# The routing gate of the last row: one load ahead of time, gated in operations of 512, in a two-layer block on one core

## The chip, the cores and the metric

The kernel runs on one core of a Trainium2 chip. Its time is the device time of one execution in microseconds (us), and runs of the same kernel are compared by their median. The core has five engines with a queue each: TensorE (PE, with its weight loads shown as PEld), VectorE (DVE), ScalarE (ACT), GpSimd (POOL) and SyncE (SP). SP computes nothing; it issues most of the transfers between device memory and the on-chip buffers.

## The reference, cut to what matters

Four rows (batch entries) of 512 tokens with 512 channels pass through two layers. Ahead of each of the four sublayers the input is gated by a bidirectional recurrence over a side input:

```python
x = x + L0_attn(L0_cond(x, f, f, w, u, cond))     # state-space mixer
x = x + L0_ffn(L0_cond2(x, f, f, w, u, cond))     # mixture of 8 experts, top 2
x = x + L1_attn(L1_cond(x, f, f, w, u, cond))     # causal attention
x = x + L1_ffn(L1_cond2(x, f, f, w, u, cond))     # dense feed-forward

# _bi_wkv(r, k, v, ...): all but the sigmoid depends on the side input only
base = sigmoid(r) * (num / maximum(den, 1e-8))
out = base * (0.8 + 0.2 * tf)

# L0_ffn: routing from the gated input, then the experts
logits = x @ gate_w.T + gate_b
top_vals, top_idx = top_k(logits, 2)
routing = softmax(top_vals)
```

So a gate (everything but `sigmoid(r)`) can be made long before its input is known. The kernel writes the sigmoid as a tanh: `h = (tanh(x / 2) + 1) * g`, where the half is in `g`.

## The kernel before, in words

Channels lie on the 128 partitions, in four chunks (`NC`), and tokens along the free dimension; a row in this form is a buffer of 128 x 4 x 512. `make_gates` computes the gates of all rows and sublayers piece by piece on DVE and ACT and stores them in device memory (`gts[l][b]`). `gated` (line 393) takes a buffer from a pool, loads a gate or a range of its tokens into it on SP's queue (line 397), and has `apply_gate` (line 379) turn it into the gated input in place: for each chunk a tanh of x on ACT into a scratch buffer `th`, then one DVE operation that adds one and multiplies (line 385).

The state-space mixer runs row by row (`for b`), within a row over four tiles of 128 tokens (`for t`). In a tile, `start_tile` computes z from the row's gated input `w.h` (line 1096), `load_sums` loads the decays `lm` (line 1126), `decays` and `outputs` do the scan, and a tile later `squares`, `norm`, `turn` and `project` (line 1244) finish it, and `add_x` (line 1260) adds the result to the row's x, for the tokens of that tile only. The gated input of rows 1 and 3 is in pool `hp` under the tag `h`, a single buffer; row 3's is read for the last time by the z matmuls of its tile 3, which are issued while tile 2 is worked on.

The routing of row b, `choose_experts` (line 605), runs during the mixer of row b + 1. It gates the row in parts into `h1` (also in `hp`, a single buffer), and for each part `logits` (line 480) computes the logits (`pl`, line 485), turns h to token rows on PE (`pht`, line 501), copies them to a scratch buffer `hr` (line 505) and stores them as `rows_h` for the experts to gather. Rows 0 to 2 are done in two parts of 256 tokens, the last row in four parts of 128, since each of its tiles becomes available only when its mixer is done. `th`, `hr` and the scratch of `route` and `order_blocks` all share one tag of the pool `tmp`, with two buffers. `route` then ranks the experts and counts; `order_blocks` lists blocks of 128 tokens of one expert.

The experts (`Experts.round`: `pg` line 788, `pn` line 799, `po` line 821, with flips `pfl` line 759 and `pyt` line 812) work on such blocks. Their first rounds, for blocks of rows 0 to 2, begin in the last tile of row 3, so that the last parts of row 3's routing, its last mixer tile and expert rounds are on PE together. After that come the remaining rounds, attention (to line 1689) and the dense feed-forward.

Order of work: the program order gives the priorities; a planner then lists the instructions of each engine in the order in which it believes them ready, by its own costs, and every engine and every queue works through its list in order. `with after(...)` and the table bookkeeping (`act.use`) only forbid some instructions to be listed before others.

Of the kernel before, what the change touches and what calls it, by code (L numbers as in the profile page):

```python
# [10 lines left out]
F32 = mybir.dt.float32  # L11
I32 = mybir.dt.int32
AF = mybir.ActivationFunctionType
ALU = mybir.AluOpType
# [3 lines left out]
P = 128  # L18
B, T, C = 4, 512, 512
NC = C // P  # L20
NT = T // P
# [61 lines left out]
def block_kernel(ctx: ExitStack, tc: tile.TileContext, a: dict, out: bass.AP):  # L83
    nc = tc.nc
# [47 lines left out]
    act = Tables()  # L132
# [9 lines left out]
    def ps_mm(name):  # L142
        return ps.tile([P, 512], F32, tag="mm", name=name, bufs=4)
# [37 lines left out]
    th = const.tile([P, B], F32, name="th")  # L181
# [32 lines left out]
    gts = [[dr.tile([P, NC, T], F32, name=f"g{l}_{b}") for b in range(B)] for l in range(4)]  # L214
# [156 lines left out]
    def pump(n=1, until=None):  # L371
        for _ in range(n):
            while until not in made and not next(making, True):
                pass
# [3 lines left out]

    def apply_gate(g, xs):

        for cc in range(NC):
            th = tmp.tile([P, T], F32, tag="th", name="th")
            n = xs.shape[-1]
            act(th[:, :n], xs[:, cc, :], AF.Tanh, scale=0.5)
            nc.vector.scalar_tensor_tensor(
                g[:, cc, :], th[:, :n], 1.0, g[:, cc, :], ALU.add, ALU.mult
            )

    def have(gate):
        while gate not in made:  # L390
            pump()

    def gated(l, b, xb, pool, part=slice(0, T), **kw):
        have((l, b))
        n = part.stop - part.start
        g = pool.tile([P, NC, n], F32, **kw)
        nc.sync.dma_start(out=g, in_=gts[l][b][:, :, part])
        apply_gate(g, xb[:, :, part])
        return g
# [202 lines left out]
        nc.vector.tensor_tensor(v2, v2, v1, ALU.mult)  # L602
        yield

    def choose_experts(b, xb, parts, pool, fine=False, **kw):

        lg = rt.tile([P, NT, E], F32, tag="lg", name="lg", bufs=2)
        nt = NT // parts
        for i in range(parts):
            h = gated(1, b, xb, pool, slice(i * nt * P, (i + 1) * nt * P), **kw)  # L610
            if fine:
                yield
            logits(h, b, lg, i * nt, nt)
            yield
        yield from route(lg, b, fine, pool, **kw)
# [258 lines left out]
    with ExitStack() as ph:  # L874
# [4 lines left out]
        hp = ph.enter_context(tc.tile_pool(name="ssm_h", bufs=1, reuse_waits="tile"))  # L879
        sm = ph.enter_context(tc.tile_pool(name="ssm", bufs=1, reuse_waits="tile"))  # L880

        def load_x(b):
            xb = (hp if b % 2 else even).tile([P, NC, T], F32, tag="x", name=f"x{b}")
            nc.sync.dma_start(out=xb, in_=a["xT"][:, b, :].rearrange("(c p) t -> p c t", p=P))
            return xb
# [35 lines left out]
        x = {0: load_x(0)}  # L921
# [164 lines left out]
        def start_tile(w, t):  # L1086
            u = Tile_()
            u.w, u.t = w, t
            u.tok = slice(t * P, (t + 1) * P)
            u.first, u.last = t == 0, t == NT - 1  # L1090

            u.zs = []
            for hh in range(2):
                pz = ps_mm("pz")
                for k in range(NC):
                    nc.tensor.matmul(
                        pz,
                        lhsT=w.h[:, k, u.tok],
                        rhs=wzt[:, k, hh * 512 : (hh + 1) * 512],
                        start=(k == 0),  # L1100
                        stop=(k == NC - 1),
                    )
                zs = sm.tile([P, 512], F32, tag="zs", name="zs", bufs=3)
                act(zs, pz, AF.Silu)
                u.zs.append(zs)
            return u
# [161 lines left out]
        def rounds(n):  # L1268
            for _ in range(n):
                if moe.i < min(NEARLY, moe.known):  # L1270
                    moe.round()
# [34 lines left out]
        routing = iter(())  # L1306
        for b in range(B):
            if b + 1 < B:
                x[b + 1] = load_x(b + 1)
            if b:  # L1310
                routing = choose_experts(
                    b - 1, x[b - 1], 2, hp, fine=True, tag="h1", name="h1", bufs=1
                )
            for t in range(NT):
                last = t == NT - 1
                exps = act.LOG_EXP
                if b == B - 1 and t >= NT - 2:
                    exps = act.EXP
                if b == B - 1 and t == NT - 2:
                    have(last_gates)  # L1320
                    for _ in making:
                        pass
                    early.close()
                    moe.open()
                    act.use(exps)
                pump(1, last_gates)
                if not last:
                    load_sums(w, t + 1, 0)
                elif b + 1 < B:
                    load_sums(following, 0, 0)  # L1330
                decays(u, 1)
                rounds(1)
                if t == NT - 2 and b + 1 < B:
                    start_scan(following)
                outputs(u, 0)
                if last and b + 1 < B:
                    more_x(following, NDI)
                with after(nc.scalar, nc.gpsimd):
                    if old is not None:
                        squares(old, 1)  # L1340
                pump(1, last_gates)
                with after(nc.vector, nc.gpsimd):
                    if old is not None:
                        norm(old)
                pump(1, last_gates)
                with after(*ENGINES):
                    if old is not None:
                        turn(old)

                if t >= 2:  # L1350
                    with after(*ENGINES):
                        next(routing, None)
                if t == NT - 3 and b + 1 < B:
                    have((0, b + 1))
                if t < 2 and b:
                    have((1, b - 1))
                if b + 1 < B or not last:
                    act.use(act.SILU)
                if t < 2:
                    with after(*ENGINES):  # L1360
                        next(routing, None)
                if t == NT - 3 and b + 1 < B:
                    following = start_row(b + 1)
                if b + 1 < B and t == NT - 2:
                    silu(following.Bc)
                    silu(following.Cc)
                if b + 1 < B and last:
                    for c in following.xc:
                        silu(c)
                nxt = None  # L1370
                if not last:
                    nxt = start_tile(w, t + 1)
                elif b + 1 < B:
                    w = following
                    nxt = start_tile(w, 0)
                act.use(exps)
                rounds(1)
                if nxt is not None:
                    start_scores(nxt)
                pump(1, last_gates)  # L1380
                with after(nc.tensor):
                    if old is not None:
                        project(old)
                if b + 1 < B and t == NT - 2:
                    with after(nc.tensor):
                        sums(following)
                if nxt is not None:
                    load_sums(w, nxt.t, 1)
                    decays(nxt, 0)
                with after(nc.scalar):  # L1390
                    if old is not None:
                        scale(old)
                outputs(u, 1)
                rounds(1)
                with after(nc.tensor, nc.vector):
                    if old is not None:
                        add_x(old)
                with after(nc.scalar, nc.gpsimd):
                    squares(u, 0)
                pump(1, last_gates)  # L1400
                with after(*ENGINES):
                    next(routing, None)
                    if b == B - 1 and t < 2:
                        next(routing)
                if b == B - 1 and t == NT - 2:
                    order_blocks(0, NEARLY)
                    moe.know(NEARLY)
                old, u = u, nxt
        act.leave()
        routing = choose_experts(B - 1, x[B - 1], 4, hp, tag="h1", name="h1", bufs=1)  # L1410
        for _ in range(NT - 1):
            next(routing)
        squares(old, 1)
# [11 lines left out]
    x = []  # L1425
    for b in range(B):
        xb = xpool.tile([P, NC, T], F32, name=f"xr{b}")
# [266 lines left out]
    with ExitStack() as ph:  # L1694
# [9 lines left out]
        for b in range(B):  # L1704
            h = gated(3, b, x[b], gp, tag="h", name=f"h3_{b}")
# [101 lines left out]
```

## Time and profile before

Three runs took 2554.86, 2562.75 and 2564.61 us.

| | us |
|---|---|
| median of the runs | 2562.75 |
| profiled execution | 2560.14 |
| its span | 2558.4 |
| mixer with gates and first routings, to about | 620 |
| row 3's routing beside the first expert rounds | 650 to 760 |
| experts, to about | 1158 |
| attention and dense feed-forward | the rest |

The profiled execution's time holds the span and what lies around it (1.7 us). A line of a timeline has the start in us from the span's start, the length, the engine, the source line, the operation and what it writes and reads; in square brackets stands the idle time before it and who ended it. A line of waits has who waited, for whom, the total in us, how often, and the longest. In the lines by stage stand the stage, its length, and then for PE, PEld, DVE, ACT and POOL the busy time and the number of instructions, the clock granted to PE, the share of the transfer engines and GB/s.

### The profile page before, as it was taken

The page shows a single profiled execution, that of the slowest core. Times are in us where ns is not written, and L with a number is a line of the kernel's source. Part 1 is how long each engine was busy: PE and PEld are TensorE (multiplying, and loading weights), DVE is VectorE, ACT ScalarE, POOL GpSimd, SP SyncE. Part 2 cuts the span into 40 slices and gives each one's busy share as a digit, 9 for nine tenths or more (in the row PEclk, how much of TensorE's full clock was granted, in tenths as well). Part 3 has the DMA queues.
Part 4 walks back from the last instruction along what each step waited for, and adds up shares of the span by engine and source line. Part 5 has one row for each costly group of instructions (what it writes and reads, how often), then busy time and mean ns, then how long its engine had stood idle before and what let it go on. Part 6 is the DMA issues. An engine that isn't in the chain of part 4 may idle for free.

```text
span 2558.4 us, 24369 instructions
## 1 busy us (share of the span) xinstructions
PE 2420.2 (95%) x8146; PEld 1288.4 (50%) x8146; DVE 1402.9 (55%) x2771; ACT 1012.0 (40%) x2074; POOL 271.9 (11%) x306
## 2 busy tenths in 40 slices
PE   3879999999999899998999999999999999999999
PEld 1545655656544444444555555555555544444444
DVE  8789999896335667646666555555444441010010
ACT  4576767667123343424544443444333331000000
POOL 4022423213211111110000000000000000000000
PEclk9989999999999999999999999999999999999999
DMA  6232524324244598775111111110000021000000
GB/s 215 71 104 71 185 75 136 120 83 153 79 169 140 195 331 319 264 262 206 58 37 46 46 33 34 46 33 9 9 17 17 17 107 46 17 4 13 9 8 17
DMA packets 88190, 243.04 MB, mean 95 GB/s; under 512 B 9472, under 2 KB 19072, under 8 KB 78976
## 3 DMA queue, kind: packets, MB, share of 16 engines
q1 hardware_dynamic: 79200, 215.78, 24.1%
q0 software_dynamic: 6560, 21.50, 2.5%
q10 hardware_dynamic: 2304, 4.20, 0.4%
q8 instruction: 65, 1.06, 0.2%
q14 instruction: 61, 0.50, 0.1%
HBM read 276.43 MB, written 46.53 MB: 126 GB/s over the span
## 4 chain that ended last, share of the span: by engine, by line
PE 49%; DVE 4%; ACT 2%; DMA 0%; issue 0%; ACTq 0%; SPq 0%; DVEq 0%
PE pd L1642 8%; PE pq L1578 7%; PE pfu L1716 6%; PE pfo L1726 6%; PE pfg L1711 6%; PE pctx L1627 5%; PE psc L1595 4%; PE pv L1564 2%; PE ptp L1618 2%; PE pk L1556 2%; DVE nmax L1600 1%; DVE psc L1598 0%; ACT pr L127 0%; DVE num L258 0%; DVE den L258 0%; DVE den L264 0%
## 5 line engine op out<-in xcount | busy, mean ns | idle before, releaser
L1578 PE MATMUL pq<-h,wq 128*128 128x512 f32 x512 | 245.3, 593 | 0.0
L1642 PE MATMUL pd<-cx,wd 128*128 128x512 f32 x512 | 222.4, 592 | 0.0
L1025 PE MATMUL pc<-h,wxb 128*128 128x512 f32 x320 | 150.3, 626 | 43.3 <-DVE h L1284 39.4
L1598 DVE TENSOR_TENSOR psc<-psc,mask 128x128 f32<-128x128 f32 x256 | 72.1, 287 | 205.2 <-PE psc L1595 205.2
L127 ACT ACTIVATE hd<-pfg,cols 128x512 f32<-128x512 f32 x44 | 30.2, 687 | 382.4 <-PE pfg L1711 382.4
L1721 DVE SCALAR_TENSOR_TENSOR hd<-pfu,cols,hd 128x512 f32<-128x512 f32 x44 | 33.0, 750 | 269.4 <-PE pfu L1716 269.3
L127 ACT ACTIVATE pr<-psc,nmax 128x128 f32<-128x128 f32 (+3 forms) x256 | 135.2, 529 | 91.8 <-DVE nmax L1600 91.4
L1716 PE MATMUL pfu<-h,ffu 128*128 128x512 f32 x352 | 158.7, 592 | 0.8 <-DMA ffu<-in_upT 0.8
L1711 PE MATMUL pfg<-h,ffg 128*128 128x512 f32 x352 | 158.9, 593 | 0.0
L788 PE MATMUL pg<-w,hT 128*128 128x512 f32 x296 | 142.6, 625 | 14.4 <-DMA w<-in_w1x 9.4
L1627 PE MATMUL pctx<-pT,v 128*128 128x512 f32 (+3 forms) x512 | 152.2, 440 | 3.9 <-ACT pT L1621 2.1
L1642 PEld LDWEIGHTS pd<-cx,wd 128*128 128x128 f32 x512 | 96.1, 190 | 114.8 <-issue 111.0
L1595 PE MATMUL psc<-kT,qT 128*128 128x128 f32 (+3 forms) x512 | 150.6, 434 | 1.6 <-ACT qT L1586 0.9
L1726 PE MATMUL pfo<-hd,ffd 128*128 128x512 f32 x352 | 151.7, 592 | 0.0
L1650 DVE TENSOR_TENSOR xr<-xr,pd 128x512 f32<-128x512 f32 x64 | 44.0, 687 | 190.8 <-PE pd L1642 190.8
L821 PE MATMUL po<-w,yT 128*128 128x512 f32 x296 | 137.0, 603 | 7.6 <-DMA w<-in_w2x 7.0
L1627 PEld LDWEIGHTS pctx<-pT,v 128*128 128x128 f32 x512 | 94.6, 191 | 92.7 <-issue 41.5
L799 PE MATMUL pn<-w,hT 128*128 128x512 f32 x296 | 133.5, 593 | 0.0
L1586 ACT ACTIVATE qT<-pq 128x512 f32<-128x512 f32 x64 | 38.2, 596 | 235.8 <-PE pq L1578 221.4
L1600 DVE TENSOR_REDUCE nmax<-psc 128x1 f32<-128x128 f32 (+3 forms) x256 | 123.7, 484 | 3.1
L1025 PEld LDWEIGHTS pc<-h,wxb 128*128 128x128 f32 x320 | 62.3, 199 | 115.8 <-issue 73.9
L1618 PEld LDWEIGHTS ptp<-ident,pr 128*128 128x128 f32 x640 | 77.3, 141 | 80.2 <-issue 38.7
(316 smaller groups left out, 4233.7 us busy)
## 6 DMA issues: line engine op xcount, KB each, us to landing
w<-in_w1x SPq DMA_DIRECT2D x76, 1024.0 KB
w<-in_w2x SPq DMA_DIRECT2D x38, 1024.0 KB
wb<-in_b1x SPq DMA_DIRECT2D x38, 512.0 KB
lm<-cs SPq DMA_DIRECT2D x32, 512.0 KB
kt<-in_fT SPq DMA_DIRECT2D x62, 256.0 KB
ek<-ek SPq DMA_DIRECT2D x62, 256.0 KB
ekv<-ekv SPq DMA_DIRECT2D x62, 256.0 KB
g<-num SPq DMA_DIRECT2D x30, 512.0 KB
```

The source lines that it names most:

```text
L127: nc.scalar.activation(*args, **kw)
L788: nc.tensor.matmul(pg, lhsT=hT[:, k, :], rhs=self.w1[s][0][:, k, :], start=(k == 0), stop=(k == NC - 1))
L821: nc.tensor.matmul(po, lhsT=yT[:, j, :], rhs=self.w2[s][:, j, :], start=(j == 0), stop=(j == NI - 1))
L1025: nc.tensor.matmul(pc, lhsT=wxb[:, k, m * P : (m + 1) * P], rhs=h[:, k, :], start=(k == 0), stop=(k == NC - 1),)
L1578: nc.tensor.matmul(pq, lhsT=u.wq[:, k, i * KVC : (i + 1) * KVC], rhs=u.h[:, k, :], start=(k == 0), stop=(k == NC - 1),)
L1595: nc.tensor.matmul(psc[:, :n], lhsT=qT[:, qi * P : n], rhs=u.kT[:, :n], start=True, stop=True)
L1600: nc.vector.tensor_reduce(nmax, psc[:, :n], AX.X, ALU.max, negate=True)
L1627: nc.tensor.matmul(pctx[:, kj * P :], lhsT=u.v[:, kj, :], rhs=pT[:, kj, kj * P :], start=(kj == 0), stop=(kj == NT - 1),)
L1642: nc.tensor.matmul(po, lhsT=u.wd[:, i, m * P : (m + 1) * P], rhs=u.ctxT[i], start=(i == 0), stop=(i == HPG - 1),)
L1711: nc.tensor.matmul(pg, lhsT=wg[:, k, cs], rhs=h[:, k, :], start=(k == 0), stop=(k == NC - 1))
L1716: nc.tensor.matmul(pu, lhsT=wu[:, k, cs], rhs=h[:, k, :], start=(k == 0), stop=(k == NC - 1))
L1726: nc.tensor.matmul(po, lhsT=wdn[:, i, m * P : (m + 1) * P], rhs=hd[i], start=(i == 0), stop=(i == NFF - 1),)
```

## The change

Two things are edited. `apply_gate` no longer goes by chunks in all cases: where a part has 256 or 128 tokens, one operation covers all four chunks of 128 tokens (a strided view of 4 x 128), so that every operation has 512 elements in a partition. A part of 256 tokens then takes two operations on each engine where it took four, a part of 128 tokens one where it took four; whole rows are treated as before.

For the last row, the gate is loaded whole (1 MB) into the buffer of tag `h` of `hp`, which row 3's own gated input held. The load is written at the end of tile 2 of row 3, after the z matmuls of tile 3 and ahead of the load of the second half of that tile's decays (`load_sums(w, nxt.t, 1)`). `choose_experts` then gates each part in place in that buffer; it takes no `h1` buffer and issues no load for this row.

```diff
     def apply_gate(g, xs):
 
-        for cc in range(NC):
+        n = xs.shape[-1]
+        for i in range(NC * n // T):
+            at = (slice(None), i) if n == T else (slice(None), slice(None), slice(i * P, (i + 1) * P))
             th = tmp.tile([P, T], F32, tag="th", name="th")
-            n = xs.shape[-1]
-            act(th[:, :n], xs[:, cc, :], AF.Tanh, scale=0.5)
-            nc.vector.scalar_tensor_tensor(
-                g[:, cc, :], th[:, :n], 1.0, g[:, cc, :], ALU.add, ALU.mult
-            )
+            tv = th if n == T else th.rearrange("p (k t) -> p k t", t=P)
+            act(tv, xs[at], AF.Tanh, scale=0.5)
+            nc.vector.scalar_tensor_tensor(g[at], tv, 1.0, g[at], ALU.add, ALU.mult)
...
-    def choose_experts(b, xb, parts, pool, fine=False, **kw):
+    def choose_experts(b, xb, parts, pool, fine=False, gate=None, **kw):
...
-            h = gated(1, b, xb, pool, slice(i * nt * P, (i + 1) * nt * P), **kw)
+            part = slice(i * nt * P, (i + 1) * nt * P)
+            if gate is None:
+                h = gated(1, b, xb, pool, part, **kw)
+            else:
+                h = gate[:, :, part]
+                apply_gate(h, xb[:, :, part])
...
                     nxt = start_tile(w, 0)
+                if b == B - 1 and t == NT - 2:
+
+                    last_gate = hp.tile([P, NC, T], F32, tag="h", name="h1_last")
+                    nc.sync.dma_start(out=last_gate, in_=gts[1][B - 1])
                 act.use(exps)
...
-        routing = choose_experts(B - 1, x[B - 1], 4, hp, tag="h1", name="h1", bufs=1)
+        routing = choose_experts(B - 1, x[B - 1], 4, hp, gate=last_gate)
```

## The prediction

> **What bounds the kernel now.** I read the page's busy table first, then the waits of TensorE (PE) in the stretch in which the last row hands over to the experts, then the timelines of PE, SyncE (SP), ScalarE (ACT) and VectorE (DVE) there, and last the lines by form.
>
> ```profile
> span 2558.4 us, 24369 instructions
> PE 2420.2 (95%) x8146; PEld 1288.4 (50%) x8146; DVE 1402.9 (55%) x2771; ACT 1012.0 (40%) x2074; POOL 271.9 (11%) x306
> ```
>
> PE is busy for 2420.2 of 2558.4 us: 138 us of idle time is all that can be won without taking PE work away, and the change takes none away. So the question is which PE idle time ends earlier. The busy time by stage around the last row shows one bad slice and a slow one after it:
>
> ```profile
> 680.00:700.00 20.00, 20.00 (x54) 9.26 (x53) 4.75 (x7) 3.73 (x8) 5.11 (x7) 1.00 0.34 121
> 700.00:720.00 20.00, 15.43 (x62) 9.00 (x61) 7.30 (x19) 3.75 (x11) 4.22 (x11) 0.94 0.45 153
> 720.00:740.00 20.00, 20.00 (x68) 11.10 (x67) 3.60 (x9) 5.76 (x12) 1.00 (x1) 0.89 0.39 145
> ```
>
> The first column after the length is PE's busy time, the third from the end the granted clock. From 700 to 720 us PE idles 4.57 us, and the clock is 0.94 and then 0.89. PE's waits from 640 to 740 us say for whom:
>
> ```profile
> PE pl L485 <- DVE h L385: 4.6, 1, 4.6
> PE pfl L759 <- DMA hb<-rows_h,idx_h: 1.8, 2, 1.4
> PE pyd L1180 <- DVE xdt L1154: 0.8, 1, 0.8
> ```
>
> One wait, 4.6 us long, of the routing logits for the gated input h. PE's timeline has it, and what follows:
>
> ```profile
> 713.60 0.42 PE L501 MATMUL pht<-ident,h 128*128 128x128 f32 x2
> 718.58 0.60 PE L485 MATMUL pl<-gw,h 128*128 128x8 f32 x2 [4.57 <-DVE h L385]
> ...
> 721.03 1.11 PE L812 MATMUL pyt<-ident,u 128*128 128x128 f32 x4
> 721.94 1.06 PE L759 MATMUL pfl<-ident,hb 128*128 128x128 f32 x4
> ...
> 725.03 0.60 PE L1235 MATMUL pyt<-ident,y 128*128 128x128 f32 x4
> ```
>
> Four transposes take 1.11 and 1.06 us just after the wait and 0.60 us at 725.03: PE runs at half speed for a while. What the logits wait for is part 2 of the last row's gate, loaded into the only h1 buffer once part 1's transposes have read it (here the lines of SP, DVE and ACT, each from its own timeline):
>
> ```profile
> 715.16 0.54 SPq L397 DMA_DIRECT2D h<-g  x1
> ```
> ```profile
> 718.23 0.49 DVE L385 SCALAR_TENSOR_TENSOR h<-th,h 128x128 f32<-128x128 f32 x2 [3.38 <-DMA h<-g]
> ```
> ```profile
> 703.37 0.58 ACT L505 COPY hr<-pht 128x512 f32<-128x512 f32 x1 [4.04 <-PE pht L501]
> 703.85 0.31 ACT L123 ACTIVATE th<-x 128x128 f32<-128x128 f32 x1
> 706.12 0.31 ACT L123 ACTIVATE th<-x 128x128 f32<-128x128 f32 x1 [1.96 <-DMA rows_h<-hr]
> ```
>
> The load takes 3.07 us from 715.16 to DVE's start at 718.23; nothing of it is covered. The ACT lines show a second queue: hr and th share a ring of two buffers, and part 1's second tanh waits until hr has been written to memory.
>
> **Part 1: the whole load, a tile ahead.** Gone are four loads of 256 KB (SP, 0.53 to 0.58 us of issue each); added is one of 1 MB. It waits for the h slot, which row 3's own input frees after the last z matmul of tile 3 (line 1096, 632.71 + 3.60 = 636.3 us). At the 319 GB/s of the page's fast slices 1 MB takes 3.3 us, and with 2.2 us around it (256 KB took 3.07 us, of which 0.8 at that rate) it lands near 642 us, an estimate. The part-0 gating starts at 656.61 us today, part 1 at 703.85, so the load has 14 us to spare. On SP the next work after its 626 us load of decays is at 649.70 (the old first load) and 657.80 us (expert weights): nothing stands behind it if it is issued at 636 us. [...] But the row shows the planner issuing by readiness: the old part-0 load (written after the experts' first round) went out at 649.70, ahead of that round's weights at 657.80. [...]
>
> When can the parts be gated? The tanh tiles come from the th ring, and its tiles seem to be handed out in the order written: part 0's first tanh ran at 656.61 us, right after the ring's last tile of the block ordering (DVE line 682, 656.01), though x of tile 0 had been ready since 624.2. So I expect no earlier start for part 0, and part 1's tanh only after part 0's hr, near 703.9, as now. From there a part is: hr 0.58, tanh 0.63 (128x512 form, line 123), gating 0.675 (128x512 form of line 385), logits 0.81, transposes 0.43, and five hand-overs of the 0.16 us that the timeline shows between ACT and DVE: 3.9 us. Two such chains (parts 1 and 2) lead to the end of part 2 near 703.4 + 7.8 = 711.2 us; today it is 721.1. They keep PE itself for 2 x 1.24 us, so 2 x 2.66 = 5.3 us must be covered, and there are the rest of pg, po and pn of the running round (2.58 + 3.44 + 3.44 = 9.5 us). **The 4.57 us wait goes.** If the cover is spent too early, up to 5.3 us come back.
>
> **The clock.** After the wait PE needs 718.58 to 725.47, 6.89 us, for 8 logits matmuls, 20 small transposes and 2 of po; by the same timeline's rows of full speed (8 logits 0.81, the 4 transposes of h 0.43, four more groups of 4 transposes at 0.44 each, po 0.86) that is 3.86 us. The row says 3.0 us lost. [...]
>
> What is late next? PE comes to the transposes of u (line 812) sooner, and u needs DVE 1.4 us after pn. Where the order has only that, PE waits 0 to 2 us; I take **+1.0**.
>
> **Part 2: gating in operations of 512.** Row 3: ACT 16 x 0.303 = 4.85 becomes 4 x 0.63 = 2.52 us, DVE 16 x 0.287 = 4.59 becomes 2.70 us; both are under 40% busy there, so nothing beyond the chain above. Rows 0 to 2, in six parts: ACT 4 x 0.410 = 1.64 becomes 1.26 us, DVE 4 x 0.420 = 1.68 becomes 1.35 us; in all 2.3 and 2.0 us. From 80 to 560 us DVE is busy 427.7 of 480 us and PE 449.4, so PE is still first; and PE's weight load waited only 0.6 us for h there. Bounds: the gain is 0 to 2.0 us; a longer operation can stand 0.26 us in front of an urgent one, 12 times, which is a loss of 3.1 us. I take **-0.6**. A strided view of 4 x 128 costs DVE no more: the residual add of that form (line 1260) takes 679 ns, like a plain one.
>
> **Sum.** 2560.1 (the profiled execution's own time, span 2558.4) - 4.6 - 3.0 - 0.6 + 1.0 = 2552.9 us. The median of the runs, 2562.75, lies 2.6 us above that execution, so I forecast **2555.5 us** for the median, 7.2 us less (0.3%). From 720 us on all is carried through: the experts' stage is paced by PE, and its weights are fetched as PE frees their buffers.
>
> **Rivals.**
> *The stall moves.* The ring chain (hr, tanh, gating) replaces the load: if PE's order puts logits 1 and 2 together, 5.3 us of wait stand there, split in two, with 0 to 3.0 us of slow clock. For it: the ring wait at 706.12 is there today. Against: 9.5 us of cover. Time: 2562.75 - 7.6 + 5.3 + 1.5 - 0.6 = 2561 (2557 to 2565).
> *More is won.* If the planner gives part 0 its ring buffers earlier, its logits (1.24 us), and perhaps part 1's, fill the holes from 653 to 662 us (PE idles 2.9 us there, and the clock is 0.84 from 660 to 680, 3.2 us). Time: 2555.5 - 2.5 - 3.0 = 2550, down to 2547.
> *Slower.* The load stands on SP ahead of the decays of tile 3's second half. They land near 640.4 (636.3 + 0.6 + 3.5, as today 626.6 to 630.15) and their eight Relus end at 642.9. ACT works in order: if its list keeps them ahead of the copies of yT (632.53), project (line 1244, 636.48) waits until 644.2: 7.7 us and 3.0 of clock, against the 7.6 won: 2566. If the old wait remains as well, or SP is held for the 14.7 us of its longest wait today, 2573 to 2580. It decides once the load is issued before 626 us; a delay of the decays alone is covered until 655.87, where PE first uses them.
>
> **How the numbers follow.** Forecast 0.55 (own range 2550 to 2559), stall moves 0.20, more is won 0.12, slower 0.13. The range 2543 to 2569 takes in the rule's price of the clock, both ends of rows 0 to 2 and the milder part of the slow case. Half a per cent, 12.8 us, is about what measurements can tell: faster means under 2550, slower over 2575.6. Of "more is won" 0.11 and of the forecast's lower end 0.08 give 0.19 for faster; the slow case's upper half and a planner that scatters the rows' order give 0.09 for slower; 0.72 between.
>
> **What would show it.** Right: no PE wait of over 2 us between 700 and 725 us, the clock near 1.0 there, one 1 MB load of h near 636 us ahead of the expert weights, part 2's logits near 710 us, all PE work after 725 us earlier by 7 us. Wrong: a new wait of logits for DVE's h or of pht for ACT's hr; decays landing at 640; a slice before 600 us that is longer than now.

## The result and the profile after

The changed kernel takes 2552.01 us (median of 7 runs, 2547.61 to 2557.70). The kernel before, run beside it and taken together with its first runs, takes 2562.26 us (7 runs). The ratio is 0.9967 with a 95% interval of 0.9953 to 0.9981, which is 8.5 us less (4.9 to 12.0); the two medians themselves lie 10.25 us apart, inside that interval. The forecast was 2555.5 us, 7.2 us less, inside half a per cent. The profiled execution of the changed kernel is its fastest, 2547.61 us, so its span must not be read as the gain. Below, stretches are compared that begin and end at the same work. The first two lines of the page:

```profile
span 2545.9 us, 24316 instructions
PE 2412.4 (95%) x8146; PEld 1283.8 (50%) x8146; DVE 1400.0 (55%) x2747; ACT 1008.1 (40%) x2050; POOL 279.3 (11%) x306
```

PE has the same 8146 matmuls; DVE and ACT have 24 instructions fewer each, as counted (12 for row 3, 12 for rows 0 to 2). The stages around the last row, with the columns of the table before:

```profile
680.00:700.00 20.00, 20.00 (x66) 10.16 (x65) 6.85 (x12) 4.66 (x10) 6.57 (x12) 1.00 0.31 106
700.00:720.00 20.00, 19.67 (x76) 10.91 (x75) 4.90 (x9) 4.56 (x9) 2.25 (x2) 1.00 0.56 184
720.00:740.00 20.00, 20.00 (x68) 10.17 (x67) 5.34 (x10) 4.20 (x7) 1.96 (x2) 1.00 0.47 177
```

Where PE was busy for 15.43 of 20 us it is busy for 19.67, and the granted clock is 1.00 where it was 0.94 and 0.89 (the same work lies about 4 us earlier here). PE's waits from 640 to 740 us no longer name DVE's h:

```profile
PE pfl L764 <- DMA hb<-rows_h,idx_h: 3.1, 2, 2.8
PE pyd L1185 <- DVE xdt L1159: 0.8, 1, 0.8
PE pxt L1155 <- DVE toks L593: 0.4, 1, 0.4
PE pyt L1240 <- ACT hT L766: 0.3, 1, 0.3
```

The wait for the gather of token rows (pfl) is now up to 2.8 us, where it was 1.4; it is at 657 us, ahead of the stretch in question. The gather is not slower: its matmuls start 4.81 us after the start of the scan matmuls before them (pyd, 652.52), where it was 4.71 us (655.87), but those took 3.34 us then and take 2.01 now. PE's timeline shows the three logits `pl` of parts 0 to 2, the transpose that stands in the place of the old wait, and the add of tile 3 (`pot`):

```profile
696.25 0.60 PE L1263 MATMUL pot<-ident,o 128*128 128x128 f32 x4
696.68 0.96 PE L485 MATMUL pl<-gw,h_last 128*128 128x8 f32 x8
...
701.45 0.95 PE L485 MATMUL pl<-gw,h_last 128*128 128x8 f32 x8
...
708.74 0.95 PE L485 MATMUL pl<-gw,h_last 128*128 128x8 f32 x8
...
712.68 0.63 PE L1240 MATMUL pyt<-ident,y 128*128 128x128 f32 x4 [0.33 <-ACT hT L766]
...
721.05 0.66 PE L1263 MATMUL pot<-ident,o 128*128 128x128 f32 x4
```

From tile 2's add to tile 3's, PE took 32.80 us before (700.54 to 733.34) and takes 24.80 now. Of these 8.0 us, 0.86 are only order: before, two of a running po's matmuls (0.43 us each) stood ahead of tile 3's add, now they stand behind it. The rest, 7.14 us, is the old wait (4.57) less the new one (0.33), and by difference 2.9 us of clock. The profile before agrees: from 718.5 to 725.5 us its granted clock is 0.57, which over 7 us is a loss of 3.0.

A second gain comes 24 us later, where the last row's counts `pcnt` are made. On PE before:

```profile
752.32 3.60 PE L799 MATMUL pn<-w,hT 128*128 128x512 f32 x8
757.66 0.38 PE L535 MATMUL pcnt<-rank,tri_lt 128*128 128x32 f32 x2 [1.74 <-DVE lg L596]
...
758.09 5.38 PE L788 MATMUL pg<-w,hT 128*128 128x512 f32 x8
```

and after:

```profile
740.89 3.60 PE L804 MATMUL pn<-w,hT 128*128 128x512 f32 x8
744.79 0.38 PE L535 MATMUL pcnt<-rank,tri_lt 128*128 128x32 f32 x2 [0.30 <-DVE lg L596]
745.01 0.39 PE L536 MATMUL pcnt<-rank,ones 128*128 128x32 f32 x2
745.23 3.68 PE L793 MATMUL pg<-w,hT 128*128 128x512 f32 x8
```

The wait is 0.30 us where it was 1.74, and the next eight matmuls take 3.68 us where they took 5.38. From the end of pn to the end of pg that is 7.55 us before and 4.42 after: 3.1 us. DVE's timeline says why. Before, u was listed ahead of the small rank operations, and DVE was held by it until pn was done:

```profile
755.96 0.69 DVE L805 SCALAR_TENSOR_TENSOR u<-pn,wb 128x512 f32<-128x512 f32 x1 [0.40 <-PE pn L799]
756.57 0.17 DVE L526 TENSOR_SCALAR is<-rank 128x32 f32<-128x32 f32 x1
756.65 0.17 DVE L527 TENSOR_SCALAR is<-rank 128x32 f32<-128x32 f32 x1
756.73 0.68 DVE L806 TENSOR_TENSOR u<-g,u 128x512 f32<-128x512 f32 x1
757.34 0.17 DVE L530 TENSOR_SCALAR rank<-rank 128x32 f32<-128x32 f32 x1
```

After, the planner has listed them the other way about. Why it did so is not shown, but the order came with the load: the kernel with the load alone (below) waits 0.30 us at the counts, the one with the operations alone 1.74.

```profile
744.16 0.18 DVE L526 TENSOR_SCALAR is<-rank 128x32 f32<-128x32 f32 x1
744.26 0.17 DVE L527 TENSOR_SCALAR is<-rank 128x32 f32<-128x32 f32 x1
744.46 0.18 DVE L530 TENSOR_SCALAR rank<-rank 128x32 f32<-128x32 f32 x1
744.56 0.18 DVE L596 TENSOR_TENSOR lg<-lg,is 128x32 f32<-128x32 f32 x1
744.66 0.68 DVE L810 SCALAR_TENSOR_TENSOR u<-pn,wb 128x512 f32<-128x512 f32 x1
```

Both gains together are seen in one stretch, from tile 2's add to the end of that pg: 62.93 us before (700.54 to 763.47), 52.66 after (696.25 to 748.91). These **10.3 us** are the measure for the experiments below; their profiles give the same stretch. After it nothing changes on the way through the experts: from there to the first keys of attention it is 395.0 us before (to 1158.5) and 394.7 after (to 1143.6). Attention and the dense feed-forward then take 1399.9 us before and 1402.3 after, with the same matmuls and the same waits. 1.4 us of this lie in the first eight matmuls of the keys, which took 5.14 us before and 6.50 after, behind equal waits of 2.35 and 2.36 us; the remaining 1.0 us is not explained here.

### The profile page after: what moved, and what is told of

It is laid out like the page before. It is cut to its first block, busy times and chain, and to the rows that moved or that the text cites. A ratio compares the mean times of both kernels' runs of the same rounds, so it can differ in the third digit from the quotient of the medians.

```text
span 2545.9 us, 24316 instructions
## 1 busy us (share of the span) xinstructions
PE 2412.4 (95%) x8146; PEld 1283.8 (50%) x8146; DVE 1400.0 (55%) x2747; ACT 1008.1 (40%) x2050; POOL 279.3 (11%) x306
## 4 chain that ended last, share of the span: by engine, by line
PE 49%; DVE 4%; ACT 2%; issue 0%; DMA 0%; ACTq 0%; SPq 0%
PE pd L1651 9%; PE pq L1587 7%; PE pfu L1725 6%; PE pfo L1735 6%; PE pfg L1720 6%; PE pctx L1636 5%; PE psc L1604 4%; PE pk L1565 2%; PE pv L1573 2%; PE ptp L1627 2%; DVE nmax L1609 1%; DVE psc L1607 0%; ACT pr L127 0%; DVE num L258 0%; DVE den L258 0%; DVE den L264 0%
```

## The experiments

Each was run beside the kernel before. "The stretch" is the one just defined, read from each profile as the end of pg less the start of tile 2's add.

### Both operation sizes, no early load

Only `apply_gate` is the changed one; the last row's gate is still loaded part by part.

```diff
+            tv = th if n == T else th.rearrange("p (k t) -> p k t", t=P)
...
         routing = choose_experts(B - 1, x[B - 1], 4, hp, tag="h1", name="h1", bufs=1)
```

> Both sizes of gating operations as in the change (256 and 128 tokens by operations of 512), but the last row's gate still loaded part by part into h1. Theory A (the load that starts only when the part before has been read is what PE waits for): the wait of logits of part 2 for DVE's h stays, 3 to 5 us between 700 and 720 us, and the slow clock after it; time 0 to 3 us under before, ratio 0.999 to 1.000. Theory B (the ring of two scratch buffers, where a tanh waits for the store of hr, sets the wait, and four tanh per part are what makes it long): the wait falls under 1.5 us without the early load, time 6 to 9 us under before, ratio 0.9965 to 0.9977.

Measured: 2564.08 us, ratio 1.0014 (1.0005 to 1.0023), 3.6 us slower than before (1.3 to 5.9). The stretch is 62.8 us. The wait is there as before, in PE's waits from 640 to 745 us:

```profile
PE pl L485 <- DVE h L387: 4.9, 1, 4.9
```

So the operations bring nothing in the last row, and cost something elsewhere.

### The early load, gating by chunks

```diff
-            th = tmp.tile([P, T], F32, tag="th", name="th")
-            tv = th if n == T else th.rearrange("p (k t) -> p k t", t=P)
+            act(th[:, :n], xs[:, cc, :], AF.Tanh, scale=0.5)
...
         routing = choose_experts(B - 1, x[B - 1], 4, hp, gate=last_gate)
```

> The whole load a tile ahead alone, gating by chunks as before (16 tanh of 128 elements for the last row). Theory A: the wait of part 2 is gone or under 1.5 us, clock 0.98 or more from 700 to 740 us, time 5 to 9 us under before, ratio 0.9965 to 0.998. Theory B: the tanh of parts 1 and 2 wait for the store of hr (2 us each time), 2 to 4 us of PE wait stay, time 0 to 4 us under before, ratio 0.9985 to 1.000.

Measured: 2548.20 us (6 runs), ratio 0.9958 (0.9944 to 0.9971). The stretch is 53.1 us, 0.4 longer than in the change. The load alone makes the whole gain in the stretch, the second part of it too.

### Operations of 512 for rows 0 to 2 only

```diff
+        fused = n == 2 * P
+        for i in range(NC * n // T if fused else NC):
...
         routing = choose_experts(B - 1, x[B - 1], 4, hp, tag="h1", name="h1", bufs=1)
```

> Operations of 512 for rows 0 to 2 only (parts of 256 tokens); the last row as before, by chunks of 128 with its four loads. The prediction's term: 0.6 us under before (from 2.0 under to 3.1 over), ratio 0.9992 to 1.001. The rival, from the two profiles, in which the add of x in row 3's tile 1 comes 3.4 us earlier although it lies ahead of the last row's gating: 3 to 5 us under before, ratio 0.998 to 0.9988. The wait at part 2 stays 4 to 5 us in both.

Measured: 2563.87 us, ratio 1.0013 (1.0003 to 1.0023), 3.3 us slower than before; stretch 63.0 us. It equals the first experiment, so what the operations cost lies in rows 0 to 2. In the two profiles the add of row 3's tile 1 comes 3.4 us earlier in the change (644.8 against 648.2 us); this run shows that the operations of rows 0 to 2 are not the reason.

### The last row only

The early load and one operation for each part of the last row; rows 0 to 2 by chunks, as before.

```diff
+        fused = n == P
+        for i in range(NC * n // T if fused else NC):
...
         routing = choose_experts(B - 1, x[B - 1], 4, hp, gate=last_gate)
```

> The whole load a tile ahead and operations of 512 for the last row; rows 0 to 2 by chunks of 256 as before. Theory A with the prediction's small term for the rows: 6.6 us under before (4 to 8), ratio 0.997 to 0.9985, about as fast as the whole change. The rival (rows 0 to 2 give 3 to 5 us): 3 to 5 us slower than the whole change.

Measured: 2545.76 us (5 runs), ratio 0.9952 (0.9939 to 0.9965), 12.3 us less than before, with the stretch at 52.7 us. Its median is the lowest of all kernels here. Its interval overlaps the change's (0.9953 to 0.9981), so this pair alone does not show that it is faster. The second gain is in it too:

```profile
746.54 3.68 PE L797 MATMUL pg<-w,hT 128*128 128x512 f32 x8
```

### The decays behind the load

This tests the rival on the other side. The change, with the decays of tile 3's second half forced behind the gate's load on SP.

```diff
                 if nxt is not None:
-                    load_sums(w, nxt.t, 1)
+                    with after(*([nc.sync] if b == B - 1 and t == NT - 2 else [])):
+                        load_sums(w, nxt.t, 1)
```

> The change, with the load of tile 3's second decays forced behind the whole gate load on SP. The prediction's slow rival: the decays land near 640 us where they landed near 630, their Relus end near 643, project starts near 644 in place of 636, and the time is 7 to 11 us over the change. The rows' reading (decays are first used by PE at 655): PE's project still starts within 1 us of where it does in the change, and the time is within 2 us of the change.

Measured: 2553.48 us, ratio 0.9973 (0.9961 to 0.9985); stretch 52.7 us. The order on SP is the feared one:

```profile
633.04 0.33 SPq L1384 DMA_DIRECT2D h_last<-g  x1
633.48 0.37 SPq L1131 DMA_DIRECT2D lm<-cs  x1
```

In the change the decays were issued at 623.43 us and the gate at 632.99. The Relus of the late half are late as the rival said, but ACT has done its copies of yT by then (the second at 629.70):

```profile
629.70 0.61 ACT L1241 COPY yT<-pyt 128x512 f32<-128x512 f32 x1
...
639.10 0.98 ACT L1144 ACTIVATE lm<-lm,cs 128x128 f32<-128x128 f32 x3 [2.86 <-DMA lm<-cs]
```

and project starts without a wait, at 633.18 us against 633.13 in the change:

```profile
633.18 7.03 PE L1249 MATMUL po<-wot,yT 128*128 128x512 f32 x16
```

The delay of the decays, 10 us, is paid by nobody. The rival needed ACT's list to keep the Relus ahead of the copies. In the change it does so for six of the eight:

```profile
627.14 1.86 ACT L1144 ACTIVATE lm<-lm,cs 128x128 f32<-128x128 f32 x6 [2.57 <-DMA lm<-cs]
628.90 0.57 ACT L127 ACTIVATE zs<-pz 128x512 f32<-128x512 f32 x1
629.38 1.04 ACT L1241 COPY yT<-pyt 128x512 f32<-128x512 f32 x2
```

With the two loads forced into the other order, the planner listed ACT anew as well and put both copies ahead of all eight. So the run shows that the planner's own lists avoid the stall, not that a late load under ACT's old list would cost nothing.

### A scratch buffer of its own for the last row's tanh

The change, with the last row's tanh in the h1 buffer, which is free now, and not in the ring that it shares with hr and the scratch of the block ordering.

```diff
-            th = tmp.tile([P, T], F32, tag="th", name="th")
+            th = own.tile([P, T], F32, tag="h1", name="thl", bufs=1)
```

> The change, with the last row's four tanh written to the h1 buffer (free once row 2's routing has used it) in place of the shared ring of scratch buffers. If the ring's order is what holds part 0's tanh until 653 us and part 1's until 699.6 us: both run before 652 us. PE's list leaves part 0's logits behind the add of tile 2 (near 697 us), so the time is that of the change within 2 us. If something else holds them, they stay where they are.

Measured: 2552.83 us, ratio 0.9969 (0.9960 to 0.9978); stretch 52.6 us. The changed kernel's ACT has part 0's tanh right after the ring's last tile of the block ordering, and part 1's after part 0's hr, 46 us later:

```profile
653.27 0.63 ACT L123 ACTIVATE th<-x 128x512 f32<-128x512 f32 x1 [4.09 <-DVE eb L688]
...
699.07 0.58 ACT L505 COPY hr<-pht 128x512 f32<-128x512 f32 x1 [4.04 <-PE pht L501]
699.55 0.63 ACT L123 ACTIVATE th<-x 128x512 f32<-128x512 f32 x1
```

With a buffer of its own the two stand close together:

```profile
654.10 0.63 ACT L123 ACTIVATE thl<-x 128x512 f32<-128x512 f32 x1 [4.81 <-PE ptok L589]
656.73 0.63 ACT L123 ACTIVATE thl<-x 128x512 f32<-128x512 f32 x1 [1.99 <-DVE h_last L390]
```

This execution is 7.7 us behind the change's at tile 1's add (652.57 against 644.84), so in the change's time these are at 646.4 and 649.0 us. The ring did set when the parts were gated. It set nothing else: PE's list keeps all logits behind tile 2's add, and the stretch is as long.

### The last row's rank operations behind u

This tests the second gain alone. The change, with the first small rank operation of the last row's route listed behind the last DVE operation of the round that was written before it, about the order of the kernel before. PE's list is the same as in the change.

```diff
+        made_before = next(i for i in reversed(nc.cur_bb.bb.instructions)
+                           if i.engine == nc.vector.engine)
...
+        with ExitStack() as es:
+            if b == B - 1:
+                es.enter_context(tc.issue_after(made_before))
+            nc.vector.tensor_scalar(i1, rank, 0.0, None, ALU.is_equal)
```

> The change, with one edge more: the first of the small DVE operations on the last row's ranks is listed behind the running expert round's last DVE operation, as it was before the change. PE's list is unchanged. If the second gain (PE waits 0.30 us for the counts in place of 1.74, and the next pg takes 3.7 us in place of 5.4) comes from DVE's new order: wait of 1.5 to 2.5 us before pcnt, pg after it over 4.5 us, time 2 to 4 us over the change. If not: time within 1 us of the change, pg after it at 3.6 us.

Measured: 2556.2 us, ratio 0.9985 (0.9974 to 0.9996); the stretch is 56.1 us, 3.5 longer than in the change. By the ratios the whole kernel is 4.6 us slower than the change, though the two intervals overlap. PE's timeline:

```profile
753.78 0.38 PE L540 MATMUL pcnt<-rank,tri_lt 128*128 128x32 f32 x2 [2.08 <-DVE g L606]
...
754.22 5.38 PE L798 MATMUL pg<-w,hT 128*128 128x512 f32 x8
```

A 2.08 us wait for DVE and a pg of 5.38 us are back. The order on DVE alone takes the second gain away, so it is what made it.

### Logits of parts 0 and 1 early

The last-row kernel with its own tanh buffer, and the first two parts of the last row's routing written at the start of tile 3, ahead of its scan, so that they could fill the holes at 653 to 662 us.

```diff
+                if b == B - 1 and last:
+                    late = choose_experts(B - 1, x[B - 1], 4, hp, gate=last_gate)
+                    for _ in range(2):
+                        next(late)
                 decays(u, 1)
```

> Load and operations of 512 for the last row only (rows 0 to 2 by chunks of 256, as before the change), the tanh in the h1 buffer, and parts 0 and 1 of the last row's routing written at the start of tile 3, ahead of the first expert rounds, so that their logits and transposes (2 x 1.24 us) stand on PE in the holes of 651 to 660 us. If those holes are empty time: 2 to 4 us under the kernel that has the last row's part alone (ratio to before 0.9935 to 0.9945), PE waits for the gather under 1.5 us. If the work only moves the expert rounds later: same as that kernel, 0.995.

Measured: 2546.79 us (6 runs), ratio 0.9948 (0.9929 to 0.9967), not to be told from the last-row kernel's 0.9952. The logits are in the holes:

```profile
655.65 1.06 PE L492 MATMUL pl<-gw,h_last 128*128 128x8 f32 x8 [0.38 <-DVE toks L600]
...
658.21 1.06 PE L492 MATMUL pl<-gw,h_last 128*128 128x8 f32 x8
```

The stretch falls from 52.7 to 50.7 us, most of the 2.5 us that these parts keep PE. But what came ahead of it grew: from tile 1's add to tile 2's it is 53.0 us (649.82 to 702.86) against 51.5 in the last-row kernel (646.07 to 697.55). PE is nearly always busy there and still slow (19.20 of 20 us, at a granted clock of 0.83; in the change this stage has 0.97, in the kernel before 0.84):

```profile
660.00:680.00 20.00, 19.20 (x72) 12.35 (x70) 4.75 (x7) 4.20 (x9) 5.69 (x8) 0.83 0.30 92
```

The profile is of the slowest of the six runs (2553.66 us), so its clock may not be that of the others. What is left by the two profiles is 0.45 us, and the intervals are too wide to tell a gain of 2 us. A hole that is filled with work which pushes other work on need not be a gain.

### Rows 0 and 1, and row 2, each alone

Both start from the last-row kernel; the first has operations of 512 for rows 0 and 1 too, the second for row 2 too.

```diff
-        fused = n == P
+        fused = n == P or (n == 2 * P and b < 2)
```
```diff
-        fused = n == P
+        fused = n == P or (n == 2 * P and b == 2)
```

> The last row as in the kernel with the early load and its parts in operations of 512; rows 0 and 1 gated for the routing in operations of 512 too, row 2 still by chunks. Ratio to before of the kernel with all rows by chunks: 0.9952; of the change, with all in 512: 0.9967 to 0.9970, some 3.3 to 4 us more. If every row's gating pays alike (a longer operation ahead of an urgent one): two thirds of it, 0.9962 (2.4 us over 0.9952). If row 2's turn of the lists is the cost (the logits and transposes no longer split among the z matmuls): 0.9952 here. If it is the lists of rows 0 and 1 (transposes of h ahead of a tile's outputs): 0.9967 to 0.9970.

> As before it, but only row 2 in operations of 512, rows 0 and 1 by chunks. If every row pays alike: one third, 0.9956. If row 2's lists are the cost: 0.9967 to 0.9970. If rows 0 and 1's: 0.9952. If both runs stand at 0.9952 the cost is not of the operations in any row but of what the rows' lists do together, or of the clock of the run.

Measured: rows 0 and 1: 2554.21 us, ratio 0.9971 (0.9962 to 0.9981). Row 2: 2552.05 us, ratio 0.9962 (0.9949 to 0.9974). Stretch 52.7 us in both. Rows 0 and 1 alone give the ratio of a kernel with all three; row 2 alone lies 2.6 us over the last-row kernel by the ratios, less than its interval. This points to rows 0 and 1 for most of the cost, but a cost shared evenly (0.9962 and 0.9956 were expected) lies in both intervals too, at the edge of the first. It isn't in the length of the operations, which in the changed kernel, up to 760 us, is what was forecast:

```profile
L387 DVE SCALAR_TENSOR_TENSOR h<-th,h 128x512 f32<-128x512 f32 x24 | 15.5, 685 | 3.7 <-DMA h<-g 2.5 <-ACT th L127 1.2
L127 ACT ACTIVATE th<-x 128x512 f32<-128x512 f32 x24 | 14.1, 624 | 9.5 <-DVE h L387 9.2 <-PE ptok L586 0.3
```

The x24 holds the 12 new operations beside the 12 of whole rows. What in the lists costs the 3 to 4 us is **still open**. PE's order up to 640 us differs between the last-row kernel and the change in four places only, by a few matmuls each (near 286, 440, 565 and 603 us); near 286 us the transposes of h stand ahead of two of a tile's scan matmuls. PE's idle time tells nothing: from 100 us to the add of row 3's tile 1 it is 27.8 to 30.8 us in the four kernels that gate rows 0 to 2 by chunks and 29.1 to 31.7 in the six that gate them in operations of 512. And single profiles don't show the cost, because rows 0 to 2 scatter by more than that from execution to execution, at the clock: that add comes at 646.1 to 649.8 us in the four and at 644.8 to 653.3 in the six. Here is the stage from 320 to 340 us, of the change and then of the kernel with rows 0 and 1:

```profile
320.00:340.00 20.00, 20.00 (x98) 12.86 (x97) 16.68 (x32) 14.05 (x27) 6.24 (x7) 1.00 0.24 80
```
```profile
320.00:340.00 20.00, 20.00 (x91) 12.86 (x91) 14.18 (x28) 11.06 (x20) 3.88 (x6) 0.85 0.26 80
```

Both gate rows 0 and 1 in operations of 512, and one has a granted clock of 1.00, the other 0.85.

## Why the prediction was right

**The wait and its clock: right.** Forecast 4.6 and 3.0 us; the runs show 4.57 and 2.9, and none of it without the load (first and third experiments). The price that the row gave for the clock held. No run shows the rule's price of the clock, which the range takes in; in its place the runs showed these 2.9 us, behind a wait of 4.57. Part 2's logits came at 708.74 us, where about 710 was said.

**The residual wait: right in sign, small.** +1.0 forecast, +0.33 measured, and for ACT's hT, not for u. Cover sufficed: PE had pg, po and pn between the logits, as counted.

**The load: right.** It went out on SP at 632.99 us (said: about 636), at the end of the last z matmuls, ahead of the expert weights at 654.74. So the slower rival did not come about: the planner did not list the load ahead of the decays. Where it was forced to list it so, ACT's list changed too and the copies of yT did not wait. In that run the decays, listed on SP behind the gate, went out at 633.48 us, right behind it (633.04), and not at 623.43.

**The ring: right.** Part 1's tanh at 699.55 us, right after hr. The rival that the stall would move there falls, since no logits waited. The rival that more is won by early logits did not come about in the change, whose logits were not early; where they were made early, no gain over the last-row kernel can be told.

**"From 720 us on all is carried through": wrong, by a gain.** This is the step that failed. The text took the lists behind the last row as they were. With the load, the planner listed the rank operations ahead of u, and 3.1 us were won at the counts. The profile before showed that wait of 1.74 us and the slow pg behind it, but the prediction's reading stopped at 740 us. It could have named the wait, though hardly that the new lists would take it away.

**Rows 0 to 2: wrong in sign.** Forecast -0.6 with a bound of +3.1 for long operations ahead of urgent ones. Measured +3.6 and +3.3 in the two kernels that have these operations and no load, at the edge of the bound. With the load, three kernels in operations of 512 (the change, decays behind, own scratch) lie at 0.9967 to 0.9973, and the three by chunks at 0.9948 to 0.9958. Whether the bound's mechanism is the cause isn't shown.

So the wait and its clock were forecast for the right reason, but the total came out near partly by luck, because two misses cancel: 7.2 forecast, and -7.1 - 3.1 + 3.5 = -6.7 by the parts (3.5 from the two kernels), with 8.5 measured (4.9 to 12.0).

## What to carry to other kernels

When lists are made by a planner, a change in one place lists other work anew. Read the waits behind the change as well as at it, and compare the lists of the kernel with each half of the change alone. Here one half was worth 11 to 12 us by itself, and the other, which saves instructions on engines that were not the limit, cost about 3.5 us by itself. The load whose buffer fell free early was the better half. Where it stood in its queue did not matter here, since nothing that was queued behind it had a user who was kept waiting.

## What the runs showed of the hardware

Behind two short waits PE was slow. In the kernel before, 1.74 us of idle time, ending at 757.66 us, were followed by eight matmuls in 5.38 us, and 2.08 us, ending at 753.78 us in the kernel with the rank operations behind u, by the same eight in 5.38; behind 0.30 us in the change they took 3.68. From 757 to 764 us the granted clock of the kernel before was 0.76. There the matmuls behind the wait took 1.70 us more than in the change, about as much again as the wait of 1.74 itself.

Not every wait of this length was followed by it. The same 16 logits matmuls, after the same idle time, in the change and then in the kernel with the rank operations behind u:

```profile
436.03 1.92 PE L485 MATMUL pl<-gw,h 128*128 128x8 f32 x16 [1.55 <-issue]
```
```profile
437.17 3.25 PE L485 MATMUL pl<-gw,h 128*128 128x8 f32 x16 [1.55 <-issue]
```

The granted clock from 434 to 442 us was 1.00 in the first and 0.72 in the second. PE's order around these matmuls is the same in both kernels. A wait of about 1.5 us thus had a price in one execution and none in the other, and the waits of 2.35 us ahead of the keys, above, cost 1.4 us more in one than in the other. What decides it is not shown. The clocks of 1.00 and 0.85 from 320 to 340 us, above, are 3.0 us apart in those 20 us: a single pair of profiles can hide a difference of that size in this kernel.
